# A two-layer pair kernel: the first stage's statistics one step earlier, the third stage without its ten-row program order

## The chip, the cores and the metric

The kernel runs on one core of one Trainium2 chip. The metric is the device time of the core in microseconds (us). The kernel before takes 3588.96 us (median of three runs, 3587.63 to 3590.16). Five engines with a queue each work side by side: TensorE (PE in the profile; PEld its weight loads), VectorE (DVE), ScalarE (ACT), GpSimd (POOL) and SyncE (SP), which here only starts transfers. An engine takes the instructions of its queue in their order; an instruction that has to wait holds those behind it.

## The reference

The input x has 384 x 384 positions of 128 channels in float32. Two layers follow each other (biases and affine parameters left out here):

```python
# layer 0
z     = layernorm(x)                                  # over the 128 channels
left  = (z @ Wl) * sigmoid(z @ Wlg)
right = (z @ Wr) * sigmoid(z @ Wrg)
core  = einsum('bikh,bjkh->bijh', left, right)
x     = x + sigmoid(x @ Wg) * (layernorm(core) @ Wout)
# layer 1
left  = x @ W_left + x @ W_eq
rsum  = sum(x @ W_right, axis=2)                      # one vector per row of positions
out   = left * rsum * sigmoid(x @ W_gate)
x     = layernorm(out @ W_out + x)
```

The kernel works in three stages. The first normalizes x, multiplies it with the four weights of layer 0 and stores the gated left and right. The second is the einsum, channel by channel, with sums for the second normalization. The third goes through the 384 rows of positions and does all that is left of layer 0 and the whole of layer 1.

## The kernel before: the parts that matter

`seq(...)` keeps an instruction in the program's order on its engine. What stands without it is ordered by a scheduler. Constants and everything else are loaded through SyncE's queue:

```python
def load(dst, src):
    nc.sync.dma_start(out=dst, in_=src)
```

First stage. A chunk is eight rows (`XR = 8`), a step four of them (`NQ = 2` steps to a chunk). Loads run six chunks ahead.

```python
NQ = XR // 4
AHEAD = NQ + 3                                        # statistics five steps ahead

def stats(n, q, half):                                # half a step: two rows
    ...
    for r in range(r0, r0 + 2):
        seq(nc.vector.bn_stats(st[:, r, :], loaded[n][:, r, :]))
    for r in range(r0, r0 + 2):
        seq(nc.vector.bn_aggr(mv[:, r, :], st[:, r, :]))
    if q == NQ - 1 and half == 1:                     # the chunk's last: 1/sqrt(var + eps)
        seq(nc.gpsimd.tensor_scalar(rs, mv[:, :, 1], EPS, 1.0, ALU.add, ALU.mult))
        seq(nc.gpsimd.tensor_tensor(rs, rs, mhalf[:, :XR], ALU.pow))
        seq(nc.gpsimd.tensor_tensor(sh, mv[:, :, 0], rs, ALU.mult))
        seq(nc.gpsimd.tensor_scalar(sh, sh, -1.0, 1.0, ALU.mult, ALU.add))

def scale(n, q):  ...   # GpSimd: four z tiles = x * rs + sh
def front(z):     ...   # TensorE: four transposes (pt); ScalarE: copy to zt
def back(n, q, zt, half):
    # TensorE: pr = zt @ wz (two rows); ScalarE: sg = sigmoid; VectorE: lr = pr * sg
    ...

for k, (n, q) in enumerate(steps):
    if k + 2 < len(steps):
        zs[k + 2] = scale(*steps[k + 2])
    for half in range(2):
        back(n, q, zt, half)
        if half == 0 and k + 1 < len(steps):
            ahead = front(zs.pop(k + 1))
        if k + AHEAD < len(steps):
            stats(*steps[k + AHEAD], half)
    zt = ahead
    ...                                               # next load of x, one store of lr
```

Third stage. `tick(t)` works on several rows at once; `r[d]` is the row that came in d ticks ago. Everything is in program order, over ten ticks (cut to the operations):

```python
if r[1]:   # pg = xT @ wg0 (PE);  gT = sigmoid(pg) (ACT)
if r[0]:   # pxt = transposes of x (PE);  xT = copy (ACT);  cs = core * rstd (POOL)
if r[10]:  # yt = py * lns (DVE);  yt += lnb (POOL)
if t >= 6 and (t - 6) % 4 == 0 and ...:
           # pq[:, :4] = wright, tot of four rows (PE);  rsum = pq + bright (DVE)
if r[2]:   # pr = cs @ wc (PE);  pr = (pr + bz) * gT (DVE);  x1T = pr + bout1 + xT, tot = its sum (DVE)
if r[6]:   # wo = wout1 * rsum (ACT)
if r[3]:   # pg2, pl = x1T @ wgate, wleft (PE);  g2 = sigmoid(pg2) (ACT);  u = (pl + bleft) * g2 (DVE)
if r[7]:   # py = u @ wo + x1T transposed, three column blocks (PE);  st, mv = statistics (DVE)
           # each second row: rs = (var + eps) ** -0.5, nm = mean * rs, rs = -rs (four on POOL)
if r[9]:   # py = py * rs + nm, three blocks (ACT)
```

Tiles that cross many ticks (x1T, u) have seven buffers, the others four. The rows' loads (x, core, rstd; four rows at a time, three buffers) and the store of the result all go through SyncE's queue.

Of the kernel before, what the change touches and what calls it, by code (L numbers as in the profile page):

```python
# [8 lines left out]
F32 = mybir.dt.float32  # L9
# [5 lines left out]
P = 128  # L15
# [4 lines left out]
def triangle_then_gated_row_kernel(ctx: ExitStack, tc: tile.TileContext, a: dict, out: bass.AP):  # L20
# [36 lines left out]
    def load(dst, src):  # L57
        nc.sync.dma_start(out=dst, in_=src)
# [19 lines left out]
    go, bo = column("L0_conv_onorm_g"), column("L0_conv_onorm_b")  # L78
    wout0, bout0 = matrix("L0_conv_Wout"), column("L0_conv_bout")
    wg0, bg0 = matrix("L0_conv_Wg"), column("L0_conv_bg")  # L80
    wleft, bleft = matrix("L1_conv_W_left"), column("L1_conv_b_left")
    weq, beq = matrix("L1_conv_W_eq"), column("L1_conv_b_eq")
    wright, bright = matrix("L1_conv_W_right"), column("L1_conv_b_right")
    wgate, bgate = matrix("L1_conv_W_gate"), column("L1_conv_b_gate")
    wout1, bout1 = matrix("L1_conv_W_out"), column("L1_conv_b_out")
    lns, lnb = const([P, C], "lns"), const([P, C], "lnb")
    load(lns, a["L1_conv_ln_scale"].partition_broadcast(P))
    load(lnb, a["L1_conv_ln_bias"].partition_broadcast(P))

# [3 lines left out]
    with tc.tile_pool(name="prep", bufs=1) as pp, tc.tile_pool(name="prep_ps", bufs=1, space=PSUM) as ps:  # L93
# [22 lines left out]
        nc.vector.scalar_tensor_tensor(wz, wcat, g0, p1, ALU.mult, ALU.add)  # L116

# [23 lines left out]
    with ExitStack() as ctx2:  # L141
# [15 lines left out]
        with tc.tile_pool(name="p1x", bufs=6) as xp, tc.tile_pool(name="p1w", bufs=3) as wp, \  # L157
# [4 lines left out]
            AHEAD = NQ + 3  # L162
# [14 lines left out]
            def stats(n, q, half):  # L177


# [9 lines left out]
                if q == NQ - 1 and half == 1:  # L189
                    seq(nc.gpsimd.tensor_scalar(rs, mv[:, :, 1], EPS, 1.0, ALU.add, ALU.mult))  # L190
                    seq(nc.gpsimd.tensor_tensor(rs, rs, mhalf[:, :XR], ALU.pow))  # L191
                    seq(nc.gpsimd.tensor_tensor(sh, mv[:, :, 0], rs, ALU.mult))
                    seq(nc.gpsimd.tensor_scalar(sh, sh, -1.0, 1.0, ALU.mult, ALU.add))
# [58 lines left out]
            for k in range(AHEAD):  # L252
                for half in range(2):
                    stats(*steps[k], half)
            zs = {k: scale(*steps[k]) for k in range(2)}
            zt = front(zs.pop(0))
            for k, (n, q) in enumerate(steps):
                ahead = None
                if k + 2 < len(steps):
                    zs[k + 2] = scale(*steps[k + 2])  # L260
                for half in range(2):
# [69 lines left out]
    with tc.tile_pool(name="p3in", bufs=3) as inp, tc.tile_pool(name="p3out", bufs=3) as op, \  # L331
         tc.tile_pool(name="p3w", bufs=4) as wp, tc.tile_pool(name="p3l", bufs=7) as lp, \
         tc.tile_pool(name="p3s", bufs=4) as sp, \
# [6 lines left out]
        def work(name, pool=wp):  # L340
            return pool.tile([P, N], F32, tag=name, name=name)

        cols = [slice(b * P, (b + 1) * P) for b in range(NB)]

        nc.vector.tensor_scalar(lns, lns, -1.0, None, ALU.mult)
        lnsb = lns.unsqueeze(1).to_broadcast([P, NB, C])
        lnbb = lnb.unsqueeze(1).to_broadcast([P, NB, C])
        loaded, rows, yts, pair, quad = {}, {}, {}, {}, {}

        def load_rows(i0):  # L350
            if i0 < N:
                xt = inp.tile([P, RG, NB, C], F32, tag="xt", name="xt")
                seq(nc.sync.dma_start(out=xt, in_=x[i0:i0 + RG].rearrange("i (b p) c -> p i b c", p=P)))
                ct = inp.tile([P, RG, N], F32, tag="ct", name="ct")
                seq(nc.sync.dma_start(out=ct, in_=core_d[i0:i0 + RG].rearrange("i h j -> h i j")))
                rt = inp.tile([P, RG, N], F32, tag="rt", name="rt")
                seq(nc.sync.dma_start(
                    out=rt.rearrange("p i j -> p (i j)"),
                    in_=rstd_d[i0:i0 + RG].rearrange("i j -> (i j)").partition_broadcast(P),
                ))  # L360
                loaded[i0] = xt, ct, rt

        D = 10

        def tick(t):

            r = [rows.get(t - d) for d in range(D + 1)]
            if r[1]:

                pg = bank("pg")  # L370
                seq(nc.tensor.matmul(pg[:, :N], lhsT=wg0, rhs=r[1]["xT"], start=True, stop=True))  # L371
                gT = r[1]["gT"] = work("gT")
                seq(nc.scalar.activation(gT, pg[:, :N], AF.Sigmoid, bias=bg0))
            if r[0]:

                pxt = bank("pxt")
                for b, s in enumerate(cols):
                    seq(nc.tensor.transpose(pxt[:, s], r[0]["x"][:, b, :], ident))  # L378
                xT = r[0]["xT"] = work("xT")
                seq(nc.scalar.copy(xT, pxt[:, :N]))  # L380
                cs = r[0]["cs"] = work("cs")
                seq(nc.gpsimd.tensor_tensor(cs, r[0]["c"], r[0]["r"], ALU.mult))  # L382
            if r[D]:

                if (t - D) % RG == 0:
                    yts[t - D] = op.tile([P, RG, NB, C], F32, tag="yt", name="yt")
                yt = yts[(t - D) // RG * RG][:, (t - D) % RG]
                seq(nc.vector.tensor_tensor(  # L388
                    yt, r[D]["py"][:, :N].rearrange("p (b c) -> p b c", b=NB), lnsb, ALU.mult
                ))  # L390
                seq(nc.gpsimd.tensor_tensor(yt, yt, lnbb, ALU.add))  # L391
            if t >= 6 and (t - 6) % 4 == 0 and (t - 6) // 4 in quad:

                q = quad[(t - 6) // 4]
                pq = bank("pq")
                seq(nc.tensor.matmul(pq[:, :4], lhsT=wright, rhs=q["tot"], start=True, stop=True))
                q["rsum"] = sp.tile([P, 4], F32, tag="rsum", name="rsum")
                seq(nc.vector.tensor_scalar(q["rsum"], pq[:, :4], bright, None, ALU.add))
            if r[2]:

                m, n = divmod(t - 2, 4)
                if n == 0:
                    quad[m] = {"tot": sp.tile([P, 4], F32, tag="tot", name="tot")}
                pr = bank("pr")
                seq(nc.tensor.matmul(pr[:, :N], lhsT=wc, rhs=r[2]["cs"], start=True, stop=True))  # L405
                seq(nc.vector.scalar_tensor_tensor(pr[:, :N], pr[:, :N], bz, r[2]["gT"], ALU.add, ALU.mult))  # L406
                x1T = r[2]["x1T"] = work("x1T", lp)
                seq(nc.vector.scalar_tensor_tensor(
                    x1T, pr[:, :N], bout1, r[2]["xT"], ALU.add, ALU.add, accum_out=quad[m]["tot"][:, n:n + 1]
                ))  # L410
            if r[6]:

                wo = r[6]["wo"] = wp.tile([P, C], F32, tag="wo", name="wo")
                m, n = divmod(t - 6, 4)
                seq(nc.scalar.activation(wo, wout1, AF.Copy, scale=quad[m]["rsum"][:, n:n + 1]))
            if r[3]:

                pg2, pl = bank("pg2"), bank("pl")
                seq(nc.tensor.matmul(pg2[:, :N], lhsT=wgate, rhs=r[3]["x1T"], start=True, stop=True))  # L419
                seq(nc.tensor.matmul(pl[:, :N], lhsT=wleft, rhs=r[3]["x1T"], start=True, stop=True))  # L420
                g2 = work("g2")
                seq(nc.scalar.activation(g2, pg2[:, :N], AF.Sigmoid, bias=bgate))
                u = r[3]["u"] = work("u", lp)
                seq(nc.vector.scalar_tensor_tensor(u, pl[:, :N], bleft, g2, ALU.add, ALU.mult))
            if r[7]:

                m, n = divmod(t - 7, 2)
# [4 lines left out]
                py = r[7]["py"] = ps2.tile([P, 512], F32, tag="py", name="py")  # L432
                for s in cols:
                    seq(nc.tensor.matmul(py[:, s], lhsT=r[7]["u"][:, s], rhs=r[7]["wo"], start=True, stop=False))  # L434
                    seq(nc.tensor.matmul(  # L435
                        py[:, s], lhsT=r[7]["x1T"][:, s], rhs=ident, start=False, stop=True, is_transpose=True
                    ))
                st = sp.tile([P, NB, 6], F32, tag="st", name="st")
                for b in range(NB):
                    seq(nc.vector.bn_stats(st[:, b, :], py[:, cols[b]]))  # L440
                for b in range(NB):
                    seq(nc.vector.bn_aggr(mv[:, n, b, :], st[:, b, :]))
                if n == 1:
                    seq(nc.gpsimd.tensor_scalar(rs, mv[:, :, :, 1], EPS, 1.0, ALU.add, ALU.mult))
                    seq(nc.gpsimd.tensor_tensor(
                        rs, rs, mhalf[:, :2 * NB].rearrange("p (a b) -> p a b", b=NB), ALU.pow
                    ))
                    seq(nc.gpsimd.tensor_tensor(nm, mv[:, :, :, 0], rs, ALU.mult))
                    seq(nc.gpsimd.tensor_scalar(rs, rs, -1.0, 0.0, ALU.mult, ALU.add))  # L449
            if r[9]:  # L450
                m, n = divmod(t - 9, 2)
                mv, rs, nm = pair[m]
                py = r[9]["py"]
                for b, s in enumerate(cols):
                    seq(nc.scalar.activation(  # L455
                        py[:, s], py[:, s], AF.Identity, bias=nm[:, n, b:b + 1], scale=rs[:, n, b:b + 1]
                    ))
# [3 lines left out]
        for t in range(N + D):  # L461
            if t < N:
# [4 lines left out]
                rows[t] = {"x": xt[:, r], "c": ct[:, r], "r": rt[:, r]}  # L467
            tick(t)
            done = t - D
            rows.pop(done, None)  # L470
            if done >= 0 and done % RG == RG - 1:
                i0 = done - RG + 1
                seq(nc.sync.dma_start(out=y[i0:i0 + RG].rearrange("i (b p) c -> p i b c", p=P), in_=yts.pop(i0)))
# [29 lines left out]
```

## Time and profile before

| | PE | DVE | ACT | POOL |
|---|---|---|---|---|
| busy, us of 3585.8 | 3496.5 | 2357.0 | 1962.6 | 1997.5 |
| first stage, 600 to 1178 us: busy us of 578 | 564.3 | 358.4 | 238.2 | 393.0 |
| second stage, 1400 to 1800 us: busy us of 400 | 400.0 | 173.1 | 149.5 | 34.6 |
| third stage, 2600 to 3000 us: busy us of 400 | 400.0 | 328.6 | 306.4 | 292.1 |

The first line is the whole span, the others are windows inside one stage. The second stage's matmuls run from 1239.9 to 2020 us. A line of the timeline gives an instruction's start, its duration, its engine and source line, its operation with output and input tiles, and in brackets how long the engine had been idle before it and what released it. Times of neighbouring matmuls overlap in the records, so the distance from start to start tells more than the durations.

### The profile page before, as it was taken

The page shows a single profiled execution, that of the slowest core. Times are in us where ns is not written, and L with a number is a line of the kernel's source. Part 1 is how long each engine was busy: PE and PEld are TensorE (multiplying, and loading weights), DVE is VectorE, ACT ScalarE, POOL GpSimd, SP SyncE. Part 2 cuts the span into 40 slices and gives each one's busy share as a digit, 9 for nine tenths or more (in the row PEclk, how much of TensorE's full clock was granted, in tenths as well). Part 3 has the DMA queues.
Part 4 walks back from the last instruction along what each step waited for, and adds up shares of the span by engine and source line. Part 5 has one row for each costly group of instructions (what it writes and reads, how often), then busy time and mean ns, then how long its engine had stood idle before and what let it go on. Part 6 is the DMA issues. An engine that isn't in the chain of part 4 may idle for free.

```text
span 3585.8 us, 48072 instructions
## 1 busy us (share of the span) xinstructions
PE 3496.5 (98%) x13646; PEld 2102.3 (59%) x13646; DVE 2357.0 (66%) x7498; ACT 1962.6 (55%) x3815; POOL 1997.5 (56%) x3526
## 2 busy tenths in 40 slices
PE   7999999999999999999999799999999999999997
PEld 3444444444444455555555477777777777777775
DVE  4666666666666544444444588888888888888886
ACT  2444444444444333333333377777777777777776
POOL 4666666666666500000000167777777777777776
PEclk9999999999999999999999899999999999999999
DMA  3675675675675288888888766666666666666662
GB/s 86 178 222 164 182 219 162 183 219 162 186 219 158 76 271 268 270 268 273 270 266 271 240 197 205 194 201 204 194 202 199 198 203 198 199 203 196 202 203 89
DMA packets 885056, 726.00 MB, mean 202 GB/s; under 512 B 18484, under 2 KB 823352, under 8 KB 884792
## 3 DMA queue, kind: packets, MB, share of 16 engines
q1 hardware_dynamic: 884792, 722.94, 65.2%
q8 instruction: 110, 1.80, 0.2%
q14 instruction: 154, 1.26, 0.1%
HBM read 437.07 MB, written 285.80 MB: 202 GB/s over the span
## 4 chain that ended last, share of the span: by engine, by line
PE 73%; POOL 16%; DVE 6%; ACT 3%; issue 2%; DMA 0%; SPq 0%; POOLq 0%; DVEq 0%; ACTq 0%
PE pc L299 22%; PE pr L233 7%; PE pr L405 7%; PE py L434 7%; PE pg L371 7%; PE pl L420 7%; PE pg L419 7%; POOL z L201 7%; POOL rs L191 7%; PE pxt L378 4%; PE py L435 3%; DVE lr L237 3%; ACT sg L235 2%; DVE st L186 2%; PE pt L210 1%
## 5 line engine op out<-in xcount | busy, mean ns | idle before, releaser
L233 PE MATMUL pr<-wz,zt 128*128 128x512 f32 x2304 | 1038.9, 594 | 0.7 <-ACT zt L212 0.7
L299 PE MATMUL pc<-lrh 128*128 128x384 f32 x2304 | 779.8, 499 | 1.4 <-DVE lr L237 1.4
L237 DVE TENSOR_TENSOR lr<-pr,sg 128x512 f32<-128x512 f32 x576 | 398.3, 691 | 471.6 <-ACT sg L235 471.6
L235 ACT ACTIVATE sg<-pr 128x512 f32<-128x512 f32 x576 | 344.0, 597 | 643.3 <-PE pr L233 327.7
L233 PEld LDWEIGHTS pr<-wz,zt 128*128 128x128 f32 x2304 | 424.1, 194 | 415.0 <-issue 414.0
L299 PEld LDWEIGHTS pc<-lrh 128*128 128x128 f32 x2304 | 446.9, 194 | 334.5 <-DVE lr L237 2.2
L455 ACT ACTIVATE py<-py,nm,rs 128x128 f32<-128x128 f32 x1152 | 495.5, 430 | 117.2 <-POOL rs L449 90.3
L201 POOL TENSOR_SCALAR z<-xt,rs,sh 128x128 f32<-128x128 f32 x1152 | 500.4, 458 | 0.0
L308 DVE TENSOR_TENSOR csum<-csum,ct 128x1152 f32<-128x1152 f32 x128 | 173.8, 1358 | 445.0 <-ACT ct L305 445.0
L290 POOL COPY lrh<-lr 128x128 f32<-128x128 f32 x256 | 68.1, 296 | 705.4 <-issue 694.4
L434 PEld LDWEIGHTS py<-wo,u 128*128 128x128 f32 x2304 | 378.5, 191 | 105.9 <-ACT py L455 2.9
L382 POOL TENSOR_TENSOR cs<-ct,rt 128x384 f32<-128x384 f32 x384 | 384.1, 1001 | 46.6 <-DMA rt<-rstd_d 40.8
L305 ACT COPY ct<-pc 128x1152 f32<-128x1152 f32 x128 | 143.3, 1120 | 486.3 <-PE pc L299 486.3
L434 PE MATMUL py<-wo,u 128*128 128x128 f32 x2304 | 404.5, 275 | 4.3 <-ACT py L455 2.7
L391 POOL TENSOR_TENSOR yt<-yt,lnb 128x384 f32<-128x384 f32 x384 | 384.0, 1000 | 5.1 <-DVE yt L388 5.1
L440 DVE BATCH_NORM_STATS2 st<-py 128x6 f32<-128x128 f32 x1152 | 266.1, 286 | 114.7 <-PE py L435 114.7
L371 PE MATMUL pg<-xT,mat_L_conv_Wg 128*128 128x384 f32 x768 | 313.3, 490 | 11.8 <-ACT xT L380 11.8
L405 PE MATMUL pr<-cs,wc 128*128 128x384 f32 x768 | 319.8, 498 | 0.0
L406 DVE SCALAR_TENSOR_TENSOR pr<-pr,bz,gT 128x384 f32<-128x384 f32 x384 | 240.2, 625 | 116.6 <-PE pr L405 116.0
L435 PE MATMUL py<-ident,x1T 128*128 128x128 f32 x1152 | 314.7, 273 | 0.0
L419 PE MATMUL pg<-x1T,mat_L_conv_W_gate 128*128 128x384 f32 x768 | 310.5, 486 | 0.0
L420 PE MATMUL pl<-x1T,mat_L_conv_W_left 128*128 128x384 f32 x768 | 310.5, 486 | 0.0
(85 smaller groups left out, 4778.1 us busy)
## 6 DMA issues: line engine op xcount, KB each, us to landing
lr_d<-lr SPq DMA_DIRECT2D x128, 1024.0 KB, 9.1
lrh<-lr_d SPq DMA_DIRECT2D x128, 768.0 KB, 4.9
xt<-in_x_dram SPq DMA_DIRECT2D x144, 512.0 KB, 5.2
core_d<-ct SPq DMA_DIRECT2D x128, 576.0 KB, 6.2
xt<-in_x_dram SPq DMA_DIRECT2D x96, 768.0 KB, 5.0
ct<-core_d SPq DMA_DIRECT2D x96, 768.0 KB, 8.8
rt<-rstd_d SPq DMA_DIRECT2D x96, 768.0 KB, 6.3
out_dram<-yt SPq DMA_DIRECT2D x96, 768.0 KB, 4.1
```

The lines of the kernel that those rows point to most:

```text
L201: seq(nc.gpsimd.tensor_scalar(z[:, r, :], xt[:, rr, :], rs[:, rr:rr + 1], sh[:, rr:rr + 1], ALU.mult, ALU.add))
L233: seq(nc.tensor.matmul(pr[:, r, :], lhsT=zt[:, 2 * half + r, :], rhs=wz, start=True, stop=True))
L235: seq(nc.scalar.activation(sg, pr[:, :, 2 * H:], AF.Sigmoid))
L237: seq(nc.vector.tensor_tensor(t[:, :, i0:i0 + 2, :], pr[:, :, :2 * H].rearrange("k i (h s) -> k h i s", s=2), sg.rearrange("k i (h s) -> k ...
L299: seq(nc.tensor.matmul(pc[:, ib, :N], lhsT=t[:, kb, ib * P:(ib + 1) * P, 0], rhs=t[:, kb, :, 1], start=(kb == 0), stop=(kb == NB - 1),))
L371: seq(nc.tensor.matmul(pg[:, :N], lhsT=wg0, rhs=r[1]["xT"], start=True, stop=True))
L405: seq(nc.tensor.matmul(pr[:, :N], lhsT=wc, rhs=r[2]["cs"], start=True, stop=True))
L419: seq(nc.tensor.matmul(pg2[:, :N], lhsT=wgate, rhs=r[3]["x1T"], start=True, stop=True))
L420: seq(nc.tensor.matmul(pl[:, :N], lhsT=wleft, rhs=r[3]["x1T"], start=True, stop=True))
L434: seq(nc.tensor.matmul(py[:, s], lhsT=r[7]["u"][:, s], rhs=r[7]["wo"], start=True, stop=False))
L435: seq(nc.tensor.matmul(py[:, s], lhsT=r[7]["x1T"][:, s], rhs=ident, start=False, stop=True, is_transpose=True))
L455: seq(nc.scalar.activation(py[:, s], py[:, s], AF.Identity, bias=nm[:, n, b:b + 1], scale=rs[:, n, b:b + 1]))
```

## The change

The first stage is given an earlier start of its statistics, so that GpSimd's root finds them ready; the constants are loaded through ScalarE's queue, those of the first product ahead of the others. At the same time the third stage is put back to its form before it was arranged by hand: no `seq`, so that a scheduler orders it; five ticks in place of ten; the row sums' product and `rsum` for each row in place of each fourth; one more small operation (nm) on VectorE and two fewer on GpSimd; and the third stage's loads, since they use `load`, through ScalarE's queue.

```diff
     def load(dst, src):
-        nc.sync.dma_start(out=dst, in_=src)
+        nc.scalar.dma_start(out=dst, in_=src)
...
-            AHEAD = NQ + 3
+            AHEAD = NQ + 4
...
-                if q == NQ - 1 and half == 1:
+
+            def powers(n, q):
+                if q == NQ - 1:
+                    _, mv, rs, sh = normed[n]
                     seq(nc.gpsimd.tensor_scalar(rs, mv[:, :, 1], EPS, 1.0, ALU.add, ALU.mult))
                     ...                                  # the same four
...
                 if k + 2 < len(steps):
                     zs[k + 2] = scale(*steps[k + 2])
+                if k + AHEAD - 1 < len(steps):
+                    powers(*steps[k + AHEAD - 1])
...
-                seq(nc.sync.dma_start(out=xt, in_=x[i0:i0 + RG]...))
+                load(xt, x[i0:i0 + RG]...)               # ct and rt likewise
...
-        D = 10
         def tick(t):
-            r = [rows.get(t - d) for d in range(D + 1)]
-            ...                                          # the order shown above
+            r0, r1, r2, r3, r4, r5 = (rows.get(t - d) for d in range(6))
+            if r1:  # pg, gT
+            if r2:
+                pl, pg2 = bank("pl"), bank("pg2")
+                nc.tensor.matmul(pl[:, N:N + 1], lhsT=wright, rhs=r2["tot"], start=True, stop=True)
+                nc.tensor.matmul(pg2[:, :N], lhsT=wgate, rhs=r2["x1T"], start=True, stop=True)
+                nc.tensor.matmul(pl[:, :N], lhsT=wleft, rhs=r2["x1T"], start=True, stop=True)
+                ...      # g2 (ACT), rsum (DVE), wo (ACT), u (DVE)
+            if r1:  # pr, then x1T and tot
+            if r3:
+                ...      # py, st, mv; each second row rs (two on POOL), then
+                nc.vector.scalar_tensor_tensor(nm, mv[:, :, :, 0], -1.0, rs, ALU.mult, ALU.mult)
+            if r0:  # pxt, xT, cs
+            if r5:  # py * rs + nm (ACT), yt = py * lns (DVE), yt += lnb (POOL)
```

The built order of the changed third stage, as TensorE's queue has it in each row: pg, the row sum's one column, pg2, pl, pr, pxt, and then py of the row whose pl has just been computed. ScalarE's queue has, in every second row, gT, g2, wo, two scalings, xT, four scalings, and in the others gT, g2, wo, xT; the scalings of two rows alternate. Of the three loads for four rows one stands behind xT, and two stand one behind the other before the last two of the six scalings.

## The prediction

> **What bounds the kernel now.** I read the page first (part 1: which engine; part 2: where stages begin), then the windows by stage, then the order in time of one period of each stage, because the busy shares cannot tell where TensorE waits.
>
> ```profile
> PE 3496.5 (98%) x13646; PEld 2102.3 (59%) x13646; DVE 2357.0 (66%) x7498; ACT 1962.6 (55%) x3815; POOL 1997.5 (56%) x3526
> ...
> PE 73%; POOL 16%; DVE 6%; ACT 3%; issue 2%; DMA 0%; SPq 0%; POOLq 0%; DVEq 0%; ACTq 0%
> ```
>
> TensorE is busy 98%, and yet GpSimd has 16% of the chain that ends last: 574 us in which TensorE does not decide. Nearly all of it (lines L201 and L191, 7% each) is in the first stage (27 to 1240 us). Its period is one chunk of eight rows, two steps of four:
>
> ```profile
> 600.23 0.60 PE L210 MATMUL pt<-ident,z 128*128 128x128 f32 x4
> 600.66 3.60 PE L233 MATMUL pr<-wz,zt 128*128 128x512 f32 x8
> 600.73 0.20 POOL L190 TENSOR_SCALAR rs<-mv 128x8 f32<-128x8 f32 x1 [2.43 <-DVE mv L188]
> 601.01 1.64 POOL L191 TENSOR_TENSOR rs<-rs,mhalf 128x8 f32<-128x8 f32 x1
> 603.20 3.47 POOL L201 TENSOR_SCALAR z<-xt,rs,sh 128x128 f32<-128x128 f32 x8
> 604.10 1.24 PE L210 MATMUL pt<-ident,z 128*128 128x128 f32 x4
> 605.17 3.60 PE L233 MATMUL pr<-wz,zt 128*128 128x512 f32 x8
> 608.61 0.60 PE L210 MATMUL pt<-ident,z 128*128 128x128 f32 x4
> ```
>
> Columns: start, duration, engine, line. The first group of transposes hands over to the matmuls after 0.43 us (600.66 - 600.23), the second after 1.07 (605.17 - 604.10): it waits for z tiles that are written one by one from 603.20, and those wait for the power (1.64 us), which waits 2.43 us for VectorE's statistics. So a chunk takes 3.87 + 4.51 = 8.38 us, of which 0.64 is that wait. The busy row hides it, since a waiting group of four still counts as busy.
>
> The second stage (1240 to 2021 us) is one unbroken row of matmuls of 779.8 us, untouched. The third has four rows as its period:
>
> ```profile
> 2600.75 0.81 PE L371 MATMUL pg<-xT,mat_L_conv_Wg 128*128 128x384 f32 x2
> 2601.40 0.49 PE L378 MATMUL pxt<-ident,xt 128*128 128x128 f32 x3
> 2601.73 0.81 PE L405 MATMUL pr<-cs,wc 128*128 128x384 f32 x2
> ...
> 2609.54 0.28 PE L396 MATMUL pq<-tot,mat_L_conv_W_right 128*128 128x4 f32 x2
> 2609.68 0.89 PE L405 MATMUL pr<-cs,wc 128*128 128x384 f32 x2
> 2610.41 0.81 PE L419 MATMUL pg<-x1T,mat_L_conv_W_gate 128*128 128x384 f32 x2
> ...
> 2616.61 0.81 PE L371 MATMUL pg<-xT,mat_L_conv_Wg 128*128 128x384 f32 x2
> ```
>
> Start to start: 0.65 us for a pair of 128x384 matmuls, 0.33 for three transposes, and nothing waits. Four rows take 15.86 us, 3.965 a row. The small product for the row sums, once in four rows, costs 0.14 + (0.73 - 0.65) = 0.22 us.
>
> **What the Trainium skill says.** "Perfetto Trace Analysis", Identifying the Most-Contended Engine: the busy share of matmuls is a poor measure of TensorE's headroom, because matmuls are pipelined. The trace agrees: 98% busy with 0.64 us of waiting in every 8.38. The same page, DMA Instruction, HWDGE: the recorded time of a DMA instruction runs from the moment its semaphores are satisfied until the sequencer is free for the next instruction. So a DMA issued by ScalarE holds ScalarE's own queue. "DMA: Bandwidth & Descriptors", Issuing engines are not separate DMA queues: issuing from another engine saves issue time on the sequencer and adds no bandwidth. No run here shows ScalarE issuing yet; on SyncE each issue in the third stage holds the queue about 0.37 us, and two in a row start 0.41 apart:
>
> ```profile
> 2617.15 0.36 SPq L355 DMA_DIRECT2D ct<-core_d  x1
> 2617.56 0.50 SPq L357 DMA_DIRECT2D rt<-rstd_d  x1
> ```
>
> **First stage.** The changed order on GpSimd is the same as before: four power instructions, eight z. What moves is VectorE: the statistics a power needs end a step (some 3.9 us) earlier, so the wait of 2.43 us goes. GpSimd's work is 2.47 (600.73 to 603.20) + 3.47 = 5.94 us a chunk, well under 7.74, so it runs ahead until the z buffers stop it. The second group should then look like the first: 2 x 3.87 = 7.74. 144 chunks x 0.64 = **-92 us**. VectorE (four times 1.31 us a chunk) and ScalarE (four times 0.60 and two of 0.58) stay below that.
>
> **Start.** Before, VectorE begins statistics at 19.6 us, after 34 constant loads and before any x load has been asked for by SyncE (13.2 us). Now x is asked for at once, but VectorE's queue still holds the weights' preparation first, and that needs the 26th constant: 0.7 + 25 x 0.47 (spacing of issues at the start) + 2 us to land + 1.3 for the small work: 15.8. **-4 us**.
>
> **Third stage.** The old form comes back, ordered by a scheduler, so I follow the built order of each engine. Per row TensorE has pg, tot (one column, now every row), pg2, pl, pr, pxt, py: 3.91 + 0.22 = 4.13 us if nothing waits. Two further things stand against it. u and wo of a row are used by py in the same tick, 1.0 us of TensorE work after pl. And ScalarE carries two rows' six scalings in every second tick, plus three DMA issues in four rows. Let pg start at 0; I use 0.85 us from a matmul pair's start to its reader (2604.66 to 2605.51), start spacings of ScalarE of 0.46 to 0.48 for 384 columns and 0.32 for 128 where no wait on itself stands between (0.43 less the 0.11 by which neighbours overlap), and 0.17 from VectorE's end to a reader on ScalarE or TensorE (rsum 2056.22 to wo 2056.39).
>
> - Tick Y (scalings). g2 can start at 0.865 + 0.85 = 1.72, ends 2.30; u 2.36 to 2.98. Now nm on VectorE: it needs GpSimd's power, whose chain (statistics after x1T, 0.9; hand-over 0.16; 0.29; power 1.33) ends about 2.98 after pg. nm ends 3.19, the two first scalings start at 3.36 and 3.68, and only then comes xT: 4.00 to 4.48. The next pg wants xT: it starts at 4.53 and not at 4.13. Slip 0.40.
> - Tick X, from 4.53. Four scalings hold ScalarE until gT at 5.64; g2 is at 6.25, on time. u ends 7.51, py could start at 7.66 anyway: 7.68. Next pg at 8.68. Two rows: 8.68.
> - In every second Y, two DMA issues (0.82) stand before the last two scalings: gT 6.46, g2 6.92, u ends 8.17, py 8.33, next pg 9.33. The third issue falls into a free stretch.
>
> Four rows: 8.68 + 9.33 = 18.0, **4.50 a row**, against 3.965: 384 x 0.535 = **+205 us**. Five ticks of draining in place of ten: about **-8** (from the last pxt at 3548.7 to the end it is now 37 us, some 24 with five; the shorter filling loses 5 of that).
>
> Sum: 3589 - 92 - 4 + 205 - 8 = **3690 us**, 2.8% slower.
>
> **Rivals.**
> - TensorE hides it all. For: sums of busy work a row are, by their new instruction counts, about 3.45 us on VectorE (3.22 plus 0.15 for rsum and 0.10 for nm) and 3.3 on ScalarE (2.97 plus 0.28), below 4.13. Against: the order is fixed in each queue, and xT stands behind scalings that wait for a power. It would be 4.13 a row: +63, and 3548 in all.
> - ScalarE's issue waits for more than the queue. ct's load also waits for GpSimd's last cs of the buffer. By the built order that product ends about 4.05 after pg, before the issue at 5.0. If it came one product (1.0 us) late, 96 issues would give some 96 us: 3786.
> - The first stage's gain is eaten by transfers. Bursts of stores fill the DMA engines now, as these windows show (last but one: DMA share):
>
> ```profile
> 634.00:668.00 34.00, 33.20 (x101) 15.69 (x99) 20.96 (x82) 14.28 (x26) 22.98 (x49) 1.00 0.92 266
> 668.00:702.00 34.00, 33.21 (x98) 15.51 (x97) 21.17 (x81) 14.28 (x26) 23.20 (x49) 1.00 0.37 106
> ```
>
>   A burst of 8 stores of 1 MB and four x loads is 10.5 MB, 39 us at 266 GB/s, and would have 31 us. For it: that does not fit. Against: the next 31 us are a third full, x is asked for six chunks ahead, and the two lr tiles leave a burst until the next begins. If it bound the bursts, half the gain would go: 3736.
> - The scalings space at 0.43 and not at 0.32: another 0.1 to 0.3 us in each pair, 3720 to 3745.
>
> **Range and chances.** The first-stage term is sure within 10 us, since one of its two steps already shows the state without the wait. The third stage is a walk by hand with some ten hand-overs; each error of 0.05 us in a tick is 19 us. Between 4.3 and 4.65 a row the total is 3613 to 3748. I take **3620 to 3745**, predicted **3690**. Faster by over 2% (below 3517) would need even less than the 4.13 of pure matmuls: 0.02. Within 2% (up to 3661, that is 4.42 a row): 0.28. Slower: 0.70.
>
> **What would show it.** First stage: both groups of transposes 0.43 us long, chunks 7.74 apart, the wait for mv gone from GpSimd, the second stage beginning near 1143. Third stage: pg waiting for xT by 0.4 us every second row, py waiting for u after the two DMA issues, ScalarE scaling waiting for nm. If TensorE shows no waits there and rows of 4.13, the walk was too slow in its hand-overs; rows above 4.7 mean a wait that I have not seen, most likely at ct's issue; chunks above 7.9 mean transfers.

## The result, and the profile after

The changed kernel takes **3652.32 us** (median of four runs, 3650.18 to 3653.78) against 3589.27 for the kernel before in the same series: 1.0176 times as long, 95% interval 1.0158 to 1.0193. That is inside the predicted range (3620 to 3745), 38 us below the predicted 3690, and on the near side of the 2% line, to which the prediction had given 0.28.

The page after, its busy row and its chain by engine:

```profile
PE 3592.0 (98%) x14222; PEld 2180.2 (60%) x14222; DVE 2383.9 (65%) x7977; ACT 1945.8 (53%) x3815; POOL 1932.0 (53%) x3142
...
PE 98%; DVE 1%; DMA 0%; ACTq 0%; POOL 0%; ACT 0%; issue 0%; POOLq 0%; DVEq 0%; SPq 0%
```

GpSimd's 16% of the chain is gone. TensorE has 576 more matmul records and 98% of the chain, and yet the kernel is slower: a chain that is all TensorE says that TensorE was always the next to go, not that it went without a gap. The timeline of the first stage (start, duration, engine, line):

```profile
560.52 0.60 PE L213 MATMUL pt<-ident,z 128*128 128x128 f32 x4
560.96 3.60 PE L236 MATMUL pr<-wz,zt 128*128 128x512 f32 x8
561.02 0.20 POOL L193 TENSOR_SCALAR rs<-mv 128x8 f32<-128x8 f32 x1 [1.82 <-DVE mv L186]
...
564.40 0.60 PE L213 MATMUL pt<-ident,z 128*128 128x128 f32 x4
564.83 3.60 PE L236 MATMUL pr<-wz,zt 128*128 128x512 f32 x8
...
568.27 0.60 PE L213 MATMUL pt<-ident,z 128*128 128x128 f32 x4
```

Both groups of transposes now hand over after 0.43 to 0.44 us, and a chunk takes 7.75 (568.27 - 560.52) and not 8.38. GpSimd still waits for VectorE, 1.82 us in place of 2.43, but it does so earlier against TensorE: the z tiles behind that wait begin at 563.49, the fourth of them would end near 565.2 (0.43 each), and the group at 564.40 has handed over by 564.83. So it works on tiles made ahead of the wait, where before it waited for those behind it. The second stage begins at 1148.56 us, 91.4 earlier than the 1239.92 of before.

The third stage, a tick with scalings and the one behind it (the lines of a wait and its waiter only):

```profile
2605.75 0.81 PE L371 MATMUL pg<-xT,mat_L_conv_Wg 128*128 128x384 f32 x2
...
2608.19 0.61 DVE L387 SCALAR_TENSOR_TENSOR u<-pl,col_L_conv_b_left,g 128x384 f32<-128x384 f32 x1
...
2608.56 0.49 PE L429 MATMUL pxt<-ident,xt 128*128 128x128 f32 x3
...
2608.72 0.15 DVE L423 SCALAR_TENSOR_TENSOR nm<-mv,rs 128x6 f32<-128x6 f32 x1
...
2608.80 1.00 POOL L432 TENSOR_TENSOR cs<-ct,rt 128x384 f32<-128x384 f32 x1 [0.16 <-PE pr L392]
2608.91 0.78 ACT L438 ACTIVATE py<-py,nm,rs 128x128 f32<-128x128 f32 x2 [0.20 <-DVE nm L423]
...
2608.95 0.46 PE L409 MATMUL py<-wo,u 128*128 128x128 f32 x2
...
2609.35 0.39 PE L409 MATMUL py<-wo,u 128*128 128x128 f32 x2
...
2609.61 0.49 ACT L431 COPY xT<-pxt 128x384 f32<-128x384 f32 x1
...
2610.14 0.30 PEld L371 LDWEIGHTS pg<-xT,mat_L_conv_Wg 128*128 128x128 f32 x2 [0.20 <-ACT xT L431]
...
2614.51 0.81 PE L371 MATMUL pg<-xT,mat_L_conv_Wg 128*128 128x384 f32 x2
```

Three things are to be seen. u ends at 2608.80, just before py can start at 2608.95; three transposes take 0.33 us before they hand over when nothing waits, here 0.39, and the first py pair takes 0.40 in place of 0.33. xT is copied behind two scalings, and the scalings behind nm, so pg's weight load waits for xT. And a tick lasts 4.39 us with scalings (2610.14 - 2605.75) and 4.37 without (2614.51 - 2610.14). Two further ticks end at 2623.26: four rows take 17.51 us, 4.378 a row, against 3.965 before.

The whole difference then closes: -91 to the end of the first stage, 384 x 0.413 = +158 in the third, and -3 because draining is 14 us shorter and filling 11 longer (read from the two traces), together +64 where +63 was measured.

### The profile page after: what moved, and what is told of

It is laid out like the page before. It is cut to its first block, busy times and chain, and to the rows that moved or that the text cites. A ratio compares the mean times of both kernels' runs of the same rounds, so it can differ in the third digit from the quotient of the medians.

```text
span 3651.0 us, 48459 instructions
## 1 busy us (share of the span) xinstructions
PE 3592.0 (98%) x14222; PEld 2180.2 (60%) x14222; DVE 2383.9 (65%) x7977; ACT 1945.8 (53%) x3815; POOL 1932.0 (53%) x3142
## 3 DMA queue, kind: packets, MB, share of 16 engines
q14 instruction: 149, 1.22, 0.1%
## 4 chain that ended last, share of the span: by engine, by line
PE 98%; DVE 1%; DMA 0%; ACTq 0%; POOL 0%; ACT 0%; issue 0%; POOLq 0%; DVEq 0%; SPq 0%
PE pr L236 27%; PE pc L306 21%; PE py L409 8%; PE pg L371 8%; PE pg L378 8%; PE pr L392 7%; PE pl L379 7%; PE pt L213 3%; PE py L410 3%; PE pxt L429 3%; PE pl L377 1%; ACTq L58 0%; DVE r L329 0%; DMA col_L_conv_b_out<-in_L_conv_b_out_dram 0%; DMA rt<-rstd_d 0%
## 5 line engine op out<-in xcount | busy, mean ns | idle before, releaser
L236 PEld LDWEIGHTS pr<-wz,zt 128*128 128x128 f32 x2304 | 416.2, 191 | 415.1 <-issue 414.2
L444 POOL TENSOR_TENSOR yt<-yt,lnb 128x384 f32<-128x384 f32 x384 | 375.8, 1000 | 395.4 <-DVE yt L441 392.5
L438 ACT ACTIVATE py<-py,nm,rs 128x128 f32<-128x128 f32 x1152 | 443.0, 437 | 46.3 <-DVE nm L423 41.8
L409 PE MATMUL py<-wo,u 128*128 128x128 f32 x2304 | 431.7, 287 | 1.6 <-DVE u L387 1.3
L409 PEld LDWEIGHTS py<-wo,u 128*128 128x128 f32 x2304 | 346.2, 190 | 42.2 <-ACT wo L385 3.0
L373 ACT ACTIVATE gT<-pg,col_L_conv_bg 128x384 f32<-128x384 f32 x384 | 225.9, 588 | 252.9 <-PE pg L371 249.7
L378 PE MATMUL pg<-x1T,mat_L_conv_W_gate 128*128 128x384 f32 x768 | 343.2, 529 | 0.0
L371 PE MATMUL pg<-xT,mat_L_conv_Wg 128*128 128x384 f32 x768 | 331.7, 514 | 1.6 <-ACT xT L431 1.6
L392 PE MATMUL pr<-cs,wc 128*128 128x384 f32 x768 | 311.8, 488 | 19.9 <-POOL cs L432 19.9
```

The source lines that it names most:

```text
L236: seq(nc.tensor.matmul(pr[:, r, :], lhsT=zt[:, 2 * half + r, :], rhs=wz, start=True, stop=True))
L371: nc.tensor.matmul(pg[:, :N], lhsT=wg0, rhs=r1["xT"], start=True, stop=True)
L378: nc.tensor.matmul(pg2[:, :N], lhsT=wgate, rhs=r2["x1T"], start=True, stop=True)
L392: nc.tensor.matmul(pr[:, :N], lhsT=wc, rhs=r1["cs"], start=True, stop=True)
L409: nc.tensor.matmul(py[:, s], lhsT=r3["u"][:, s], rhs=r3["wo"], start=True, stop=False)
L438: nc.scalar.activation(py[:, s], py[:, s], AF.Identity, bias=r5["nm"][:, b:b + 1], scale=r5["rs"][:, b:b + 1])
```

## The experiments

The theories. For the first stage: the place of GpSimd's root in its queue, one step behind the statistics it reads, brings the gain (A, where an expectation uses letters; against it: the sixth step of lead does). For the third: the row sums' product of each row costs the 64 us that it occupies TensorE; and the waits beside it come from transfers started by ScalarE, from rsum behind the whole of pl in one PSUM tile (C), or from xT behind scalings that wait for a power. Where an expectation names a run, e1 is the first one below, e4 the one with the loads on SyncE, and e6 the first by hand. Every ratio is against the kernel before in the same series (3588.89, 3585.21 and 3587.42 us in the three series, in this order: the first four kernels, the next four, the last four).

### The first stage alone

After's first stage and constants, before's third stage.

> The changed first stage and constants, with the third stage of before (ten ticks, program order, its loads on SyncE). If the two halves of the change simply add: 3589 - 92 (144 chunks x 0.64 us) - 1 (first transposes 1.05 us earlier) = 3496 us, chunks 7.74 us apart. Rival: the gain of the first stage is partly won only because the third stage changed too (transfers on two queues): then above 3510.

3499.28 us, ratio 0.9749 [0.9734, 0.9764]. The first stage brings 89.6 us, and the third stage of the change gives 153.0 back. This version beats both kernels.

### Six ahead, the root at once

```diff
-                if k + AHEAD - 1 < len(steps):
-                    powers(*steps[k + AHEAD - 1])
                 ...                        # back, front, stats
+                if k + AHEAD < len(steps):
+                    powers(*steps[k + AHEAD])
```

> As e1, but the root is put into GpSimd's queue at once after its statistics, as before, and only the statistics stay six steps ahead. Theory A (the place of the root in GpSimd's queue is what counts: the z tiles of the next transposes stand behind a root that waits for statistics not yet done): the wait of 0.64 us a chunk stays, chunks 8.38 apart, 3588 us. Rival B (six steps ahead is what counts): chunks 7.74 apart, 3496 us.

3590.55 us, 1.0002 [0.9993, 1.0010]: the whole gain is gone although the statistics run six steps ahead and the constants still come through ScalarE's queue.

```profile
600.00 1.22 PE L213 MATMUL pt<-ident,z 128*128 128x128 f32 x4
601.06 3.60 PE L236 MATMUL pr<-wz,zt 128*128 128x512 f32 x8
...
605.00 0.20 POOL L193 TENSOR_SCALAR rs<-mv 128x8 f32<-128x8 f32 x1 [2.44 <-DVE mv L186]
```

The second group of transposes lasts 1.22 us and hands over after 1.06 again, and the root waits 2.44 us. More lead moves the statistics and the instruction that waits for them together.

### Five ahead, the root one step behind

```diff
-            AHEAD = NQ + 4
+            AHEAD = NQ + 3
```

> As e1, but the statistics only five steps ahead as before, and the root one step behind them. Theory A (place of the root): 3496 us, chunks 7.74 apart. Rival B (six steps ahead): most of the wait comes back, 3570 to 3590 us.

3498.57 us, 0.9747 [0.9732, 0.9762], the same as with six. That the root stands one step behind the statistics it reads is all of it; the sixth step is not needed.

### Before, with the row sums' product in each row

```diff
-            if t >= 6 and (t - 6) % 4 == 0 and (t - 6) // 4 in quad:
+            if r[3]:
-                seq(nc.tensor.matmul(pq[:, :4], lhsT=wright, rhs=q["tot"], start=True, stop=True))
+                seq(nc.tensor.matmul(pq[:, :1], lhsT=wright, rhs=r[3]["tot"], start=True, stop=True))
```

> The kernel before, with the row sums' product and rsum for every row in place of every fourth, everything else in its ten-tick order. If the product costs what it showed (0.22 us of TensorE each, 0.165 us a row more) and nothing waits: 4.13 us a row, 3589 + 63 = 3652 us. Rival: TensorE has slack for it in the weight loads: 3600 us or less. Rival: the extra PSUM tile in each tick brings waits for banks: above 3680 us.

3652.94 us, 1.0176 [1.0159, 1.0193]: +64.05 us, which is 384 x 0.167 where the working of the prediction has 4.13 - 3.965 = 0.165. With the ten-tick order nothing else waits, and a row takes 4.13. It has as many matmul records as the changed kernel (14222), so the 0.25 us a row that the changed kernel takes beyond 4.13 comes of waits in its order of operations and not of more work for TensorE. That this kernel is as slow as the changed one is chance: it has no first-stage gain.

### The third stage's loads on SyncE

```diff
-                load(ct, core_d[i0:i0 + RG]...)         # xt and rt likewise
+                nc.sync.dma_start(out=ct, in_=core_d[i0:i0 + RG]...)
```

> The changed kernel, with only the third stage's loads back on SyncE; the order of all computing instructions is the same. Theory of the prediction (a DMA issue holds ScalarE, 0.82 us for two before the last two scalings, 0.65 us of it on TensorE's path in four rows): 3652 - 62 = 3590 us. Rival from the trace (ScalarE's sequencer issues while ScalarE still computes, some 0.16 us in four rows): 3637 to 3652 us.

3652.97 us against 3652.32, and four rows take 17.51 us in both traces: nothing. Starting transfers from ScalarE costs this stage no time. The changed kernel's trace shows why, in the tick with two of them:

```profile
2618.36 0.49 ACT L431 COPY xT<-pxt 128x384 f32<-128x384 f32 x1
...
2618.59 0.37 ACTq L58 DMA_DIRECT2D ct<-core_d  x1
...
2618.73 0.45 ACT L438 ACTIVATE py<-py,nm,rs 128x128 f32<-128x128 f32 x1
...
2618.99 0.52 ACTq L58 DMA_DIRECT2D rt<-rstd_d  x1
```

ACTq is the sequencer, ACT the engine. The issue of ct begins while xT is still being computed, and the next scaling starts in the middle of it, 0.37 us behind xT's start, exactly as in the tick without transfers (2609.61 to 2609.98). ScalarE does lose something further on. Here are pg and gT behind the tick without transfers, and behind the tick with two:

```profile
2610.14 0.91 PE L371 MATMUL pg<-xT,mat_L_conv_Wg 128*128 128x384 f32 x2
...
2611.35 0.61 ACT L373 ACTIVATE gT<-pg,col_L_conv_bg 128x384 f32<-128x384 f32 x1
...
2618.90 0.91 PE L371 MATMUL pg<-xT,mat_L_conv_Wg 128*128 128x384 f32 x2
...
2620.26 0.58 ACT L373 ACTIVATE gT<-pg,col_L_conv_bg 128x384 f32<-128x384 f32 x1
```

gT comes 1.36 us behind pg in place of 1.21; with the loads on SyncE it is 1.21 in both. So two issues hold ScalarE up by some 0.15 us, not by 0.82, and u still starts 0.92 us behind pl in every tick: the delay does not reach TensorE.

### The row sum in another PSUM tile

rsum waits for the whole of pl, since both lie in one tile (316.1 us of waiting in all); here its column goes to py's tile.

```diff
-                nc.tensor.matmul(pl[:, N:N + 1], lhsT=wright, rhs=r2["tot"], start=True, stop=True)
+                py2 = r2["py"] = ps2.tile([P, 512], F32, tag="py", name="py")
+                nc.tensor.matmul(py2[:, N:N + 1], lhsT=wright, rhs=r2["tot"], start=True, stop=True)
```

> The changed kernel, with the row sum's one column written into py's tile and not into pl's, so that rsum needn't wait for pl. Theory C (rsum waits for the whole of pl and stands in front of u, so that u ends too late by some 0.08 us and TensorE waits at py and cannot preload u, 0.13 us in each row): 3652 - 50 = 3602 us. Rival D (u waits for g2 or pl anyway, at the same moment): 3640 to 3655 us.

3680.20 us, 1.0258 [1.0242, 1.0273]: 28 us slower than the changed kernel, outside both expectations. rsum is early now (0.31 us behind its product), and in the tick with scalings u still starts 0.91 us behind pl (0.92 before the edit), so the shared tile was not what held u. As wo is ready earlier, the scheduler places it ahead of g2 on ScalarE. A tick without scalings and the end of the one behind it:

```profile
2658.18 0.81 PE L380 MATMUL pl<-x1T,mat_L_conv_W_left 128*128 128x384 f32 x2
...
2659.17 0.62 DVE L388 SCALAR_TENSOR_TENSOR u<-pl,col_L_conv_b_left,g 128x384 f32<-128x384 f32 x1 [0.46 <-ACT g L382]
...
2663.75 0.49 PE L430 MATMUL pxt<-ident,xt 128*128 128x128 f32 x3
...
2664.08 0.46 PE L410 MATMUL py<-wo,u 128*128 128x128 f32 x2
```

In the tick without scalings u now waits for g2 and starts 0.99 to 1.11 us behind pl, the later figure behind two transfers. In the tick with scalings nm comes 3.02 us behind pg in place of 2.97. Pairs of rows take 8.90 us in place of 8.755, of which each of the two ticks gives about half; no run separates the two causes. One thing got better: in the tick with scalings the transposes hand over to py after 0.33 us again, with u as late as before. So lateness of u alone does not make the 0.39 of the changed kernel, where py waits for wo as well.

### The third stage by hand, in the scheduler's order

The third stage written with `seq`, each engine's compute instructions in the order that the scheduler had given them, loads on SyncE; only cs is made one row ahead and not several.

> The changed kernel's third stage written in the order in which the scheduler put it, all of it in program order, loads on SyncE: a reference for the next two. Same order, so the time of e4 within 10 us.

3797.09 us, 1.0589 [1.0573, 1.0605], 144 us slower than the run with loads on SyncE: a miss. The timeline of this kernel in a tick with scalings:

```profile
2706.68 1.00 POOL L423 TENSOR_TENSOR cs<-ct,rt 128x384 f32<-128x384 f32 x1
2706.78 0.92 DVE L403 SCALAR_TENSOR_TENSOR nm<-mv,rs 128x6 f32<-128x6 f32 x1
...
2707.73 0.78 ACT L371 ACTIVATE py<-py,nm,rs 128x128 f32<-128x128 f32 x2 [0.96 <-DVE nm L403]
...
2708.97 0.91 PE L384 MATMUL pg<-xT,mat_L_conv_Wg 128*128 128x384 f32 x2 [0.73 <-ACT xT L422]
```

nm, six numbers a partition, lasts 0.92 us in place of 0.15 and ends with GpSimd's cs, which began 0.10 us before it. In the changed kernel cs waited for pr and began 0.08 us after nm (2608.80 and 2608.72). The next pg comes 5.15 us after its forerunner (2703.82 to 2708.97), 0.76 more than 4.39; 192 pairs x 0.76 = 146 us, the whole miss. The Trainium skill, "SBUF — State Buffer", Who interferes with whom, says that VectorE and GpSimd share a pair of ports as an exclusive lock, which a VectorE instruction with two SBUF inputs needs as well, and that the order of issue decides who blocks. Both traces agree with it.

### xT ahead of all six scalings

```diff
-            scalings(six[:2])
             seq(nc.scalar.copy(xT, pxt[:, :N]))
-            scalings(six[2:])
+            scalings(six)
```

> As e6, with xT ahead of all six scalings on ScalarE. Theory E (the next pg waits for xT because two scalings that wait for nm stand in front of it, 0.12 us of waiting and 0.10 of exposed weight load in every second row): e6 - 20 to - 42 us; the lower figure if the six scalings in a row then delay g2 by 0.1 us. Rival (TensorE is held by u alone): no change.

3688.07 us, 1.0280 [1.0265, 1.0296]: 109 below the run before where 20 to 42 were expected, since pg no longer waits for what waits for nm. But nm still lasts 0.91 us in the mean and now holds x1T behind it on VectorE, so this says nothing yet of the place of xT alone.

### Other forms of cs and nm

Three kernels. The first, with the factor rstd of cs left out:

```diff
-                seq(nc.gpsimd.tensor_tensor(cs, r0["c"], r0["r"], ALU.mult))
+                seq(nc.gpsimd.tensor_scalar(cs, r0["c"], 1.0, 0.0, ALU.mult, ALU.add))
```

> The hand-ordered third stage (3797.09 us), with GpSimd's product of core and rstd (two inputs in SBUF) replaced by a scaling of the core alone (one input); the factor rstd is left out. If nm's 0.92 us comes of two instructions with two SBUF inputs each sharing a port, nm goes back to 0.15 us and the kernel to about 3650 (+-20). If any GpSimd instruction beside nm is enough to hold it up, nm stays as long as GpSimd's scaling lasts and the time stays near 3797 or above.

3651.43 us, 1.0178 [1.0161, 1.0195]: the changed kernel's time to within 1.5 us, by hand. The next two leave the factor mean out of nm, once in the order with two scalings ahead of xT and once with xT first:

```diff
-                seq(nc.vector.scalar_tensor_tensor(nm, mv[:, :, :, 0], -1.0, rs, ALU.mult, ALU.mult))
+                seq(nc.vector.tensor_scalar(nm, rs, -1.0, 0.0, ALU.mult, ALU.add))   # rs: every second element
```

> The hand-ordered third stage (3797.09 us) with nm on VectorE made from one SBUF input: minus rs, without the factor mean (left out), still waiting for the power; the powers lie in every second element so that the reading is strided. If nm was held up because it reads two SBUF inputs beside GpSimd's work, it is 0.15 us or less again and the kernel near 3650 (+-20). If any VectorE instruction without a PSUM input is held up beside that GpSimd product, it stays near 0.9 us and 3797.

> The same one-input nm (factor mean left out) in the hand-ordered third stage that copies xT ahead of all six scalings (3688.07 us with the two-input nm). Without the clash the two differ in the place of xT alone. If pg's wait for xT behind two scalings is what the changed kernel's tick with scalings loses, this run is below the one with xT behind two scalings by about 0.1 to 0.3 us a pair of rows (20 to 60 us), with no wait for xT left. If the wait is paid elsewhere anyway (u after g2 behind the scalings), both are the same within 10 us.

3801.07 and 3686.91 us, 1.0594 [1.0578, 1.0610] and 1.0277 [1.0262, 1.0292]: no better than with two inputs. The second was to isolate the place of xT, but as the clash stayed, it did not. The timelines, first of the kernel with the one-input cs, then of the one with the one-input nm:

```profile
2711.43 0.15 DVE L403 SCALAR_TENSOR_TENSOR nm<-mv,rs 128x6 f32<-128x6 f32 x1
2711.44 0.52 POOL L423 TENSOR_SCALAR cs<-ct 128x384 f32<-128x384 f32 x1
```

```profile
2706.57 1.00 POOL L423 TENSOR_TENSOR cs<-ct,rt 128x384 f32<-128x384 f32 x1
2706.67 0.93 DVE L403 TENSOR_SCALAR nm<-rs 128x6 f32<-128x6 f32 x1
```

With nm at 0.15 us the hand-written stage loses all of its 146 us, so nm's hold-up was the whole miss. That one input to cs is not the reason can be seen in the same run. In the lines above, cs begins 0.01 us behind nm, and not 0.10 ahead. Four times, early in the stage, it begins ahead:

```profile
1992.89 0.51 POOL L423 TENSOR_SCALAR cs<-ct 128x384 f32<-128x384 f32 x1
1992.95 0.46 DVE L403 SCALAR_TENSOR_TENSOR nm<-mv,rs 128x6 f32<-128x6 f32 x1
```

There nm takes 0.46 us and ends with cs, though cs has one input; in the 185 ticks in which nm begins first it takes 0.16, and so it does once where both begin together. So it is the order of the two starts that decides, and a shorter cs only makes the hold-up shorter. That fits the same section of the skill: the first to start keeps the ports, and a VectorE `tensor_scalar` may take them with one input, too.

### xT first, and nm on GpSimd

The whole computation; nm and the negated rs on GpSimd behind the power, as in the kernel before, xT ahead of the six scalings.

```diff
-                seq(nc.vector.scalar_tensor_tensor(nm, mv[:, :, :, 0], -1.0, rs, ALU.mult, ALU.mult))
                 ...                                  # behind the power:
+                    seq(nc.gpsimd.tensor_tensor(nm, mv[:, :, :, 0], rs, ALU.mult))
+                    seq(nc.gpsimd.tensor_scalar(rs, rs, -1.0, 0.0, ALU.mult, ALU.add))
```

> Whole computation: xT ahead of all six scalings, and nm and the negated rs made on GpSimd right behind its power, as in the kernel before, so VectorE has no nm. The clash of nm with cs is gone; the scalings start some 0.5 us later than with a 0.15 us nm, but they are behind xT anyway. Expected 3600 to 3640, below the changed kernel's 3652. If the later scalings keep ScalarE from gT and g2 of the next row, u and py are late and the gain is gone: 3650 to 3690.

3648.62 us, 1.0170 [1.0155, 1.0185]: 4 us from the changed kernel where 12 to 52 were expected. Its timeline, from pg behind a tick with scalings:

```profile
2703.91 0.81 PE L385 MATMUL pg<-xT,mat_L_conv_Wg 128*128 128x384 f32 x2
...
2705.42 0.62 ACT L387 ACTIVATE gT<-pg,col_L_conv_bg 128x384 f32<-128x384 f32 x1
...
2706.55 0.62 DVE L401 SCALAR_TENSOR_TENSOR u<-pl,col_L_conv_b_left,g 128x384 f32<-128x384 f32 x1
2706.72 0.49 PE L417 MATMUL pxt<-ident,xt 128*128 128x128 f32 x3
...
2707.31 0.46 PE L431 MATMUL py<-wo,u 128*128 128x128 f32 x2
...
2708.38 0.81 PE L385 MATMUL pg<-xT,mat_L_conv_Wg 128*128 128x384 f32 x2
...
2712.64 0.81 PE L385 MATMUL pg<-xT,mat_L_conv_Wg 128*128 128x384 f32 x2
```

The tick with scalings is 4.26 us (2712.64 - 2708.38) and has no wait for xT. But all six scalings now stand before the next row's gT, which starts 1.51 us behind pg (0.85 where ScalarE is free); u is late, and py comes 0.59 us behind pxt in place of 0.39. That tick takes 4.47. The scalings start right behind xT (2711.72 and 2712.09), so nm, which comes later from GpSimd, does not hold them. The pair is 8.73 where the changed kernel has 8.755: the wait has changed its place, not its size.

## Why the prediction was right, and where it was not

It held in its range because its large terms were right and its errors partly cancelled, which is luck in part: 62 us of the sum stood for a delay that does not reach TensorE, and the other terms came out 25 us worse than predicted.

| Term | predicted, us | shown, us |
|---|---|---|
| first stage with the start | -92 - 4 | -91 (second stage's begin), -89.6 (run alone) |
| row sums' product in each row | +63 (of the 205) | +64 |
| waits on xT and u, without transfers | +81 (of the 205) | +95 |
| two transfers ahead of scalings | +62 (of the 205) | 0 |
| drain and filling | -8 | -3 |

The third-stage rows are in us of 96 times four rows: 8.68 + 8.68 - 16.52 = 0.84 predicted for the waits, 17.51 - 16.52 = 0.99 shown.

- **First stage: right, step by step.** 0.43 us for both groups, 7.75 a chunk where 7.74 was predicted. One sign was wrong: GpSimd's wait for mv did not go, it became 1.82 us and harmless. And the cause can be said more sharply than "a step earlier": with the root at once the statistics are earlier too, and nothing is gained; what counts is that the root reads those of the step before.
- **Start: mis-sized, 1 us for 4.** Statistics start at 18.56 us (19.60 before). SyncE's first load of x starts only at 11.38 us, not "at once". But VectorE stands 6.39 us in the weights' preparation, up to 18.17: it waits for a product of TensorE, and that waits for the 26th constant, which is issued at 11.95 us and lets TensorE start at 16.72, 4.8 us later, where the prediction took 2. (There are 28 constant loads, not 34.)
- **The step that failed: "two DMA issues (0.82) stand before the last two scalings".** It took the issue's record for time of the engine. The run with the loads on SyncE shows 0 where this step has 62 us, and the trace a delay of ScalarE by 0.15 us for two issues. "Perfetto Trace Analysis", DVE / Act Engine Instruction, has what the prediction should have set beside the DMA section it used: a compute instruction is pushed to a wait queue, and the sequencer is free for the next while the engine works. The trace agrees: the scaling at 2618.73 starts inside the issue recorded from 2618.59 to 2618.96.
- **Tick with scalings: right in kind, too long.** A wait for xT behind two scalings behind nm is there. nm starts 2.97 us behind pg (2.98 predicted), but lasts 0.15 and hands over in 0.04, where 0.21 and 0.17 were taken; the scalings start at 3.16 and not 3.36. The tick is 4.39, not 4.53.
- **Tick without: too short, 4.37 for 4.15.** "py could start at 7.66 anyway" left no cost for weights that come just in time. py loses 0.06 + 0.07 us in every tick, waiting for u and wo (transposes 0.39 for 0.33, first py pair 0.40 for 0.33), and late xT leaves pg's first weight load uncovered: 0.75 us from pg to the row sums' product (2610.14 to 2610.89) where it takes 0.65 otherwise. Per four rows: 4 x 0.13 + 2 x (0.13 + 0.10) = 0.98, the measured 0.99; the other 0.13 is what pg of the tick with scalings slips.
- **The rivals.** TensorE hides all (3548) falls: a tick without any wait on xT, in the last experiment, is still 4.26, not 4.13. Waiting at ct's issue, transfers eating the first stage's gain, and scalings spaced at 0.43 each predicted more than came (3786, 3736, 3720 and up); the runs show none of them, and neighbouring scalings start 0.35 us apart in the changed kernel, near the 0.32 that was taken.
- **The chances.** Two per cent lay at 4.42 us a row by the prediction's own sum; the row is 4.378. So the outcome held likelier, over 2% slower (0.70), did not come. Taking the DMA step out of the working gives 3628 and would have put "within 2%" first.

## What to carry to other kernels

An instruction that waits holds its whole queue, so place it one step behind what it waits for: that move alone is worth 90 us here, and the version with the root one step behind, the constants on ScalarE's queue and the ten-tick third stage kept (3498.57 us) is the one to use. Results that TensorE uses in the tick that makes them (u, wo) cost 0.13 us a row here although they came almost in time; some rows of distance, as in the kernel before, hide that. Before a wait is moved, ask what stands behind it: with xT put first, ScalarE's six scalings held up gT in its place.

## What the runs showed that was not expected

- A VectorE instruction on 128 x 6 elements took 0.92 us in place of 0.15, because a GpSimd product had started 0.10 us before it; a GpSimd scaling with one input held it as well, for 0.46 us, when it started first. That cost 144 us of the kernel, and the order of instructions within each engine had hardly changed: the gap between the two starts turned from +0.08 to -0.10 us.
- Issues of transfers on a busy ScalarE cost the kernel nothing measurable: 3652.32 us with 288 of them, 3652.97 without. Two in a row, 0.37 and 0.52 us long, delayed ScalarE by 0.15 us.
- The GpSimd scaling of one input took 0.52 us for 128 x 384 where the product of two takes 1.00.
